# Attention over 32 graphs on one core: a schedule planned with other landings and durations, two plain projections and a fifth buffer

## The chip, the core and the metric

The kernel runs on one core of a Trainium2 chip. TensorE (PE) multiplies matrices into the eight PSUM banks, ScalarE (ACT) and VectorE (DVE) work on tiles in SBUF and read PSUM, GpSimd (POOL) and SyncE (SP) issue DMA transfers. Each engine runs its own queue of instructions strictly in order. The metric is the device time of one execution in microseconds, the median over several; lower is better.

## The reference

There are 32 graphs of 512 nodes with 512 features, each with an adjacency matrix of integers. For each graph the kernel computes a layer norm over the features and a ReLU, then two graph attention layers, and adds the input as residual. Layer 1 has four heads of 256 features, joined, with a bias and an ELU; layer 2 has one head of 512.

```
h   = relu(layernorm(x))
xl  = h @ W                                  # split into heads
e   = leaky_relu(xl·a_src [source] + xl·a_dst [target], 0.2)
att = softmax over sources of (e where adj > 0 or on the diagonal, else -1e9)
out = att^T @ xl + b
x + layer2(elu(layer1(h)))
```

All data are float32.

## The kernel before

The matrices are cut into 128 rows. Per graph and layer there are two matrix stages: the *projection* (`project1`: 512 x 512 by 512 x 1024; `project2`: 512 x 1024 by 1024 x 512, each with extra columns that give the attention scores) and the *gather* (attention weights times projected features).

**Block products.** Most of these products use a scheme with seven products of half-sized blocks instead of eight (`sevens`, L734, and `gather1`, L921). It needs sums of blocks ahead of the matmuls: `sums` (L693) makes four on DVE from the left operand (`ht` in layer 1, `h1` in layer 2), three of which lie in `hs`; `sums_of_weights` (L346) makes four of the weights, once, in slots 3 to 6 of `w1_sb` and `w2_sb`. One of them overwrites the weight block in slot 6. The results are put together after the matmuls: `minus` (L721) copies the first product of a block out of PSUM on ACT and subtracts the others on DVE. The first graph's `project1_first` (L797) and the first graphs' gathers (`gather1_plain`, L853) are plain: eight block products, that is a sum over all of the inner dimension in one PSUM bank, then one copy. With 258 columns a plain layer-1 projection is 64 matmuls where the other has 56; layer 2 has the same numbers at 257 columns.

**Softmax.** `Soft.columns` (L577) takes the score columns, spreads one of them over all partitions by two small DMAs through DRAM (`spread`: `das<-as`, `as<-das`). `Soft.first` (L596) makes, for four row tiles, a leaky ReLU on ACT, a masked minimum on DVE, an exponential with its sum on ACT; the logarithm of the sums goes through DRAM in the same way (`drr<-rr`, `rr<-drr`). `Soft.second` (L640) makes the weights `p` on DVE, adds the mask (by an accumulating DMA from POOL's queue, `p<-dm`, or by a DVE add for the first graph's first three heads and the last graph) and takes the exponential on ACT. The masks `m` are one tile; `masks` (L441) makes the next graph's after the last reader, and transposes them by DMA.

**Other steps.** `norm_turn` (L490) applies the norm on ACT and turns the tile: an ACT copy into an `adj` buffer, a DMA transpose, an ACT copy into `ht`. `elu` (L841) uses one tile of the buffers `xrs` (four of them, L297) for an exponential and a ReLU on ACT, then one DVE instruction writes `h1`. `residual` (L1012) loads x into `xrs` tiles and adds the bias b2 by an accumulating DMA; for graph 30, whose tiles lie elsewhere, by a DVE add with the copy of b2 in `b2_sb` (L287, L405). `gather2` (L1055) adds its products onto those tiles and writes them out.

**Order.** Nothing is issued as it is written. Every step is a job of class `Program` (L45) with an engine, a planned cost, what it reads and writes, and for a DMA its size. `order` (L169) plans with these costs: PE's jobs keep the order in which they are written; all other engines' jobs are ranked by how late they may run, found by planning backwards and forwards twelve times, and the plan with the earliest end is issued. A DMA of a size is planned to land after

```
landed = max(landed, t + jobs[j][1] + self.DMA_LEAD) + jobs[j][4] / self.DMA_RATE
r = landed + self.DMA_TAIL
```

with `DMA_LEAD, DMA_TAIL, DMA_RATE = 1.2, 1.0, 280e3` (L53; us, us, bytes per us). The planned order is fixed in the program; on the chip each engine waits at the head of its queue for what it needs.

The opening, in the order in which PE's jobs are written: `project1_first` for graph 0 (L1129), `project1` for graph 1 (L1146), the four heads of graph 0's gather (L1149), `project2` for graph 0 (L1163). The loop from L1169 then runs, per turn i, gather 1 of graph i+1 in two halves, `project1` of graph i+2 and gather 2 of graph i around it, and `project2` of graph i+1.

Of the kernel before, what the change touches and what calls it, by code (L numbers as in the profile page):

```python
# [10 lines left out]
F32 = mybir.dt.float32  # L11
# [8 lines left out]
P = 128  # L20
# [24 lines left out]
class Program:  # L45
# [6 lines left out]
    CROSS, SAME = 0.15, 0.1  # L52
    DMA_LEAD, DMA_TAIL, DMA_RATE = 1.2, 1.0, 280e3  # L53

# [155 lines left out]
def tile_gat(  # L210
# [75 lines left out]
    b1_sb = sbuf.tile([P, 2, FT], F32, name="b1_sb")  # L286
    b2_sb = sbuf.tile([P, DO], F32, name="b2_sb")  # L287
    part = sbuf.tile([P, 2, FT, 2], F32, name="part")
# [7 lines left out]
    adjs = slots("adj", 2, [P, N], I32)  # L296
    xrs = slots("xr", 4, [P, N])  # L297
    ls = slots("l", 3, [P, N])
# [95 lines left out]
    def weights2():  # L394

        for (r, c), ix in AT.items():
            dma(
                512e3, [("ht", 0, 0)], [("w2", ix)], w2_sb[:, ix, :, 1 - c : W2H - c],
                w2[r * HF // 2 : (r + 1) * HF // 2, c * DO // 2 : (c + 1) * DO // 2].rearrange(
                    "(k p) f -> p k f", p=P  # L400
                ),
            )
        dma(4e3, (), ["b1"], b1_sb[:, 0], b1.rearrange("(c p) -> p c", p=P))
        dve(TINY, ["b1"], ["b1"], nc.vector.tensor_scalar_mul, b1_sb[:, 1], b1_sb[:, 0], -1.0)
        dma(256e3, (), ["b2"], b2_sb, rows_of(b2, P))  # L405
        for a, v in enumerate((as2, ad2)):
            lk, bc = ls.take()
            dma(256e3, (), [lk], bc, rows_of(v[0], P))
            for (r, c), ix in AT.items():
                for k in range(KH):  # L410
                    jk, junk = xrs.take()
                    dve(
                        0.4, [lk, ("w2", ix)], [("part", a, r, c, k), jk],
                        nc.vector.scalar_tensor_tensor,
                        junk[:, : DO // 2], w2_sb[:, ix, k, 1 - c : W2H - c], 1.0,
                        bc[:, c * DO // 2 : (c + 1) * DO // 2], op0=OP.mult, op1=OP.mult,
                        accum_out=part[:, a, r * KH + k, c : c + 1],
                    )
                    xrs.give(jk)
            ls.give(lk)  # L420
        for a in range(2):
            for r in range(2):
                g = part[:, a, r * KH : (r + 1) * KH, :]
                col = slice(0, 1) if a == 0 else slice(W2H - 1, W2H)
                dve(
                    TINY, [("part", a, r, c, k) for c in range(2) for k in range(KH)],
                    [("w2s", AT[r, a])], nc.vector.tensor_add,
                    w2_sb[:, AT[r, a], :, col], g[:, :, 0:1], g[:, :, 1:2],
                )
# [60 lines left out]
    def norm_turn(b, t):  # L490
# [3 lines left out]
        act(  # L494
            0.62, [xk, sk + (t,)], [xk], hn, hn, AF.Relu,
            bias=st[:, t, S : S + 1], scale=st[:, t, S + A : S + A + 1],
# [13 lines left out]
        else:  # L510
# [3 lines left out]
            act(  # L514
                1.14, [xk], [ak], words.rearrange("p (h f) -> p h f", h=2),
                hn.bitcast(U16).rearrange("p (f h) -> p h f", h=2), AF.Copy,
# [9 lines left out]
            act(  # L526
                1.14, [xk], [("ht", t, 0), ("ht", t, 1)],
                ht[:, :, t * P : (t + 1) * P].bitcast(U16).rearrange("p k (n h) -> p h k n", h=2),
# [205 lines left out]
    def sevens(left, right, rkeys, put, kh, units, width, order):  # L734
# [3 lines left out]
        for u, n in order:  # L738
            m = units[u][0]
            acc, first = {1: "a", 2: "g", 5: "b", 6: "a", 7: "a", 3: "b", 4: "a"}[n], n in (1, 2, 5)  # L740
            if first:
# [4 lines left out]
            pe(  # L746
                akeys + rkeys(n), [bk], kh * width / 597,
                [
# [48 lines left out]
    def project1_first(zt):  # L797

        for j in range(H // 2):
            zk, z = zt[j]  # L800
            for t in range(NT):
                for c in range(2):
# [5 lines left out]
                           for q in (("w1", AT[r, c], k), ("w1s", AT[r, c], k, j))],  # L808
                        [bk], KT * 0.435,
                        [  # L810
# [9 lines left out]
                    banks.give(bk)  # L820
                yield

    def project1(b, left):
# [97 lines left out]
    def gather1(soft, j):  # L921
# [4 lines left out]
        for i, n in PAIR:  # L926
# [5 lines left out]
            if first:  # L932
# [4 lines left out]
            pe(  # L937
                akeys + wkeys, [bk], KQ * M / 597,
                [
# [37 lines left out]
    def project2(b, left):  # L977
# [18 lines left out]
        )  # L996

    def scores_2(b):
        def cols(z, i, zk):
# [12 lines left out]
    def residual(b, places=(xrs,) * NT):  # L1012

        XR[b] = []
        for d in range(NT):
# [6 lines left out]
            dma(256e3, (), halves, xr, x[b, d * P : (d + 1) * P, :])  # L1022
            if places[0] is xrs:
                accumulate(256e3, [xk], halves, xr, rows_of(b2, P))
            else:
                dve(0.59, [xk, "b2"], halves, nc.vector.tensor_add, xr, xr, b2_sb)
            XR[b].append((places[d], xk, xr))
# [74 lines left out]
    def run(products):  # L1102
        for _ in products:
            pass
# [7 lines left out]
    S1, S2 = {}, {}  # L1112
    PLAIN = 1
    HT_KEYS = [("ht", t, c) for t in range(NT) for c in range(2)]
# [13 lines left out]
    for t in range(NT):  # L1128
        norm_turn(1, t)  # L1129
    sums_of_weights(w1_sb, w1_keys, 1.2)  # L1130
    left1 = sums(ht_blocks(), KQ, 0.59)
    s = S1[0] = Soft(0, 1, lambda z, i, zk: [zk + (0, c, t) for c in range(2) for t in range(NT)])
# [9 lines left out]
    masks(1)  # L1142
    run(project1(1, left1))
    weights2()
# [15 lines left out]
    s.first(3)  # L1160
    sums_of_weights(w2_sb, lambda ix: [("w2", ix), ("w2s", ix)], 1.15)
    left2 = sums(h1_blocks(), KH, 1.15)
    run(project2(0, left2))  # L1163
    for t in range(NT):
# [98 lines left out]
```

## Time and profile before

| | us |
|---|---|
| median of 4 runs | 2869.75 (2866.93 to 2876.84) |
| the profiled execution | 2868.61 |
| its span | 2866.6 |
| TensorE busy | 2774.9 (97%) |
| VectorE busy | 2585.0 (90%) |
| ScalarE busy | 2305.6 (80%) |
| GpSimd busy | 417.7 (15%) |
| mean granted TensorE clock | 0.993 |

The profile shows one execution. "Busy" of TensorE includes matmuls that run at a lower granted clock. "Idle before" a group is the time in which its engine did nothing, and the releaser is what ended that time; names such as `mm<-w_sb,hs` read output from inputs, with buffer numbers left out (`mm` is a PSUM bank). All steps recorded by one helper carry one line: L316 is ACT, L319 DVE, L322 SP's DMAs, L327 POOL's accumulating DMAs, L333 the matmuls. A 128x512 tile of float32 is 256 KB.

### The profile page before, as it was taken

Reading aid. Unit: us, or ns where it says so; the run is one execution under the profiler, and the core shown is the slowest. Engines: PE = TensorE matmul, PEld = TensorE weight load, DVE = VectorE, ACT = ScalarE, POOL = GpSimd, SP = SyncE. Lnnn points to the kernel's source line nnn. Section 1 sums busy time; section 2 is a strip of 40 time slices with the busy share of each in tenths; the row PEclk is TensorE's granted clock in tenths of the full one; section 3 lists DMA queues with packets and bytes.
Section 4 is the critical chain, followed back from the end, with each engine's and each line's share of the span. In section 5 each row is a group of like instructions: output and inputs, shape, how many; then the busy total and the mean of one; then the engine's idle time right before and its main releaser. Section 6 shows DMA issues by size and latency. Waiting matters only on the chain. (4 is left out here: it accounts for less than half of the span.)

```text
span 2866.6 us, 41534 instructions
## 1 busy us (share of the span) xinstructions
PE 2774.9 (97%) x12456; PEld 2362.5 (82%) x12456; DVE 2585.0 (90%) x6567; ACT 2305.6 (80%) x4861; POOL 417.7 (15%) x466
## 2 busy tenths in 40 slices
PE   7999999999999999999999999999999999999997
PEld 6668888888888888888888878888888888888875
DVE  7979998989989989999989989999998999999995
ACT  6878797888878788887888778888888788888872
POOL 0011111111111111111111111111111111111100
PEclk9999999999999999999999999999999999999999
DMA  6577787687776777877787867778767788787724
GB/s 204 151 170 186 184 202 188 181 192 196 180 201 177 181 196 195 203 190 183 187 184 185 208 164 188 195 186 208 188 176 192 180 202 197 188 199 186 188 66 130
DMA packets 389455, 527.23 MB, mean 184 GB/s; under 512 B 227184, under 2 KB 231280, under 8 KB 389232
## 3 DMA queue, kind: packets, MB, share of 16 engines
q1 hardware_dynamic: 327600, 332.68, 41.6%
q0 software_dynamic: 61632, 191.92, 30.9%
q8 instruction: 99, 1.62, 0.2%
q14 instruction: 124, 1.02, 0.1%
HBM read 344.72 MB, written 50.79 MB: 138 GB/s over the span
## 5 line engine op out<-in xcount | busy, mean ns | idle before, releaser
L333 PE MATMUL mm<-w_sb,hs 128*128 128x257 f32 (+1 forms) x3024 | 694.1, 383 | 23.6 <-ACT xl L316 14.8
L333 PEld LDWEIGHTS mm<-w_sb,hs 128*128 128x128 f32 x3024 | 572.8, 191 | 119.8 <-ACT xl L316 26.9
L327 POOL DMA_DIRECT2D p<-dm x304 | 268.1, 883 | 2046.2 <-DVE p L319 1030.4
L316 ACT ACTIVATE l<-as,z 128x512 f32<-128x512 f32 x640 | 441.8, 723 | 111.4 <-DMA as<-das 103.5
L316 ACT ACTIVATE p<-p,z 128x512 f32<-128x512 f32 x640 | 432.7, 722 | 112.1 <-DMA p<-dm 78.5
L316 ACT ACTIVATE l<-l,low 128x512 f32<-128x512 f32 x640 | 459.4, 723 | 72.3 <-DVE low L319 70.4
L319 DVE SCALAR_TENSOR_TENSOR p<-rr,z 128x512 f32<-128x512 f32 x640 | 457.6, 744 | 45.3 <-DMA rr<-drr 45.0
L333 PE MATMUL mm<-p,xl 128*128 128x256 f32 (+1 forms) x2016 | 488.5, 390 | 7.3 <-ACT p L316 5.9
L333 PE MATMUL mm<-w_sb,ht 128*128 128x258 f32 x2112 | 481.5, 382 | 4.1 <-ACT xl L316 3.1
L333 PE MATMUL mm<-w_sb,h 128*128 128x257 f32 x2056 | 470.0, 380 | 6.3 <-DVE h L319 4.3
L319 DVE CUSTOM_DVE_ANT_1 l<-l,mt 128x512 f32<-128x512 f32 x640 | 426.8, 682 | 42.8 <-ACT l L316 40.6
L333 PEld LDWEIGHTS mm<-w_sb,ht 128*128 128x128 f32 x2112 | 400.4, 190 | 66.1 <-ACT xl L316 6.1
L333 PEld LDWEIGHTS mm<-p,xl 128*128 128x128 f32 x2016 | 381.7, 190 | 83.9 <-issue 19.1
L333 PEld LDWEIGHTS mm<-w_sb,h 128*128 128x128 f32 x2056 | 389.9, 190 | 65.7 <-DVE h L319 5.3
L316 ACT ACTIVATE xl<-mm 128x258 f32<-128x258 f32 (+2 forms) x752 | 282.1, 384 | 54.3 <-PE mm L333 52.2
L319 DVE TENSOR_TENSOR xl<-xl,mm 128x258 f32<-128x258 f32 x558 | 224.1, 417 | 34.6 <-PE mm L333 25.6
L316 ACT ACTIVATE h<-mm 128x256 f32<-128x256 f32 x480 | 175.1, 379 | 76.5 <-PE mm L333 75.9
L316 ACT ACTIVATE xr<-h,b_sb 128x512 f32<-128x512 f32 x240 | 171.5, 723 | 80.9 <-DVE h L319 80.5
L333 PE MATMUL mm<-t,hs 128*128 128x256 f32 x960 | 217.7, 379 | 0.9 <-DVE hs L319 0.7
L333 PEld LDWEIGHTS mm<-t,hs 128*128 128x128 f32 x960 | 182.1, 190 | 26.7 <-DVE hs L319 1.1
L319 DVE TENSOR_TENSOR xr<-mm,xr 128x256 f32<-128x256 f32 (+1 forms) x424 | 170.6, 416 | 32.2 <-PE mm L333 19.3
L319 DVE SCALAR_TENSOR_TENSOR h<-h,b_sb,xr 128x512 f32<-128x512 f32 x240 | 175.7, 744 | 19.8 <-ACT xr L316 19.0
(105 smaller groups left out, 3427.3 us busy)
## 6 DMA issues: line engine op xcount, KB each, us to landing
p<-dm POOLq DMA_DIRECT2D x304, 512.0 KB, 5.1
rr<-drr SPq DMA_DIRECT2D x160, 512.0 KB
x<-in_x_dram SPq DMA_DIRECT2D x129, 256.0 KB
adj<-in_adj_dram SPq DMA_DIRECT2D x128, 256.0 KB
as<-das SPq DMA_DIRECT2D x64, 512.0 KB
xr<-in_x_dram SPq DMA_DIRECT2D x124, 256.0 KB
xr<-in_L_gnn_b_dram POOLq DMA_DIRECT2D x124, 256.0 KB, 6.0
out_dram<-xr SPq DMA_DIRECT2D x124, 256.0 KB
```

Of the source, the lines that this page charges most:

```text
L316: prog.add("ACT", cost, reads, writes, lambda: nc.scalar.activation(*a, **k))
L319: prog.add("DVE", cost, reads, writes, lambda: f(*a, **k))
L327: lambda: nc.gpsimd.dma_start(to, at, accum_op=OP.add), 1.4 * size,
L333: f(*a, **k)
```

## The change

- `DMA_TAIL` is 1.3 instead of 1.0, and the planned costs of three ACT steps and of the matmuls are other numbers.
- Graph 1's layer-1 projection and graph 0's layer-2 projection are plain: `project1_plain` and `project2_plain`. The block sums of `ht` and `h1` for these two go; the sums of the weights are written after them.
- `b2_sb` is gone, with its load; `residual` adds b2 by an accumulating DMA for every graph. `xrs` has five tiles instead of four.

```diff
-    DMA_LEAD, DMA_TAIL, DMA_RATE = 1.2, 1.0, 280e3
+    DMA_LEAD, DMA_TAIL, DMA_RATE = 1.2, 1.3, 280e3
...
-    b2_sb = sbuf.tile([P, DO], F32, name="b2_sb")
...
-    xrs = slots("xr", 4, [P, N])
+    xrs = slots("xr", 5, [P, N])
...
-        dma(256e3, (), ["b2"], b2_sb, rows_of(b2, P))
...
-            0.62, [xk, sk + (t,)], [xk], hn, hn, AF.Relu,
+            0.71, [xk, sk + (t,)], [xk], hn, hn, AF.Relu,
...
-                1.14, [xk], [ak], words.rearrange("p (h f) -> p h f", h=2),
+                0.96, [xk], [ak], words.rearrange("p (h f) -> p h f", h=2),
...
-                1.14, [xk], [("ht", t, 0), ("ht", t, 1)],
+                1.21, [xk], [("ht", t, 0), ("ht", t, 1)],
...
-                akeys + rkeys(n), [bk], kh * width / 597,
+                akeys + rkeys(n), [bk], kh * width / 593,
...
-                        [bk], KT * 0.435,
+                        [bk], KT * 0.437,
...
+    def project1_plain():
+
+        for j in range(H // 2):
+            for c in range(2):
+                h = 2 * j + c
+                for t in range(NT):
+                    bk, bt = banks.take()
+                    pe(
+                        [("ht", t, 0), ("ht", t, 1)]
+                        + [q for r in range(2) for k in range(KQ)
+                           for q in (("w1", AT[r, c], k), ("w1s", AT[r, c], k, j))],
+                        [bk], KT * 0.437,
+                        [
+                            (mm, (bt[:, :W], ht[:, k, t * P : (t + 1) * P],
+                                  w1_sb[:, AT[k // KQ, c], k % KQ, j, :]),
+                             dict(start=(k == 0), stop=(k == KT - 1)))
+                            for k in range(KT)
+                        ],
+                    )
+                    act(
+                        COPY, [bk], [("xl", t, h, i) for i in range(FPH)], xl[:, t, h, :], bt[:, :W],
+                        AF.Copy, scale=-1.0,
+                    )
+                    banks.give(bk)
...
-                akeys + wkeys, [bk], KQ * M / 597,
+                akeys + wkeys, [bk], KQ * M / 593,
...
+    def project2_plain():
+
+        for t in range(NT):
+            for c in range(2):
+                bk, bt = banks.take()
+                for k in range(FT):
+                    ix = AT[k // KH, c]
+                    pe(
+                        [("h1", k, t // 2), ("w2", ix), ("w2s", ix)], [bk], 0.437,
+                        [(mm, (bt[:, :W2H], h1[:, k, t * P : (t + 1) * P], w2_sb[:, ix, k % KH, :]),
+                          dict(start=(k == 0), stop=(k == FT - 1)))],
+                    )
+                act(
+                    COPY, [bk], [("xl2", t, c)], xl2[:, t, c * W2H : (c + 1) * W2H], bt[:, :W2H],
+                    AF.Copy, scale=-1.0,
+                )
+                banks.give(bk)
...
-            if places[0] is xrs:
-                accumulate(256e3, [xk], halves, xr, rows_of(b2, P))
-            else:
-                dve(0.59, [xk, "b2"], halves, nc.vector.tensor_add, xr, xr, b2_sb)
+            accumulate(256e3, [xk], halves, xr, rows_of(b2, P))
...
-    PLAIN = 1
+    PLAIN, PLAIN_A, PLAIN_C = 1, True, True
...
-    sums_of_weights(w1_sb, w1_keys, 1.2)
-    left1 = sums(ht_blocks(), KQ, 0.59)
+    if not PLAIN_A:
+        sums_of_weights(w1_sb, w1_keys, 1.2)
+        left1 = sums(ht_blocks(), KQ, 0.59)
...
-    run(project1(1, left1))
+    if PLAIN_A:
+        project1_plain()
+    else:
+        run(project1(1, left1))
...
-    left2 = sums(h1_blocks(), KH, 1.15)
-    run(project2(0, left2))
+    w2_keys = lambda ix: [("w2", ix), ("w2s", ix)]
+    if PLAIN_C:
+        project2_plain()
+        sums_of_weights(w2_sb, w2_keys, 1.15)
+    else:
+        sums_of_weights(w2_sb, w2_keys, 1.15)
+        left2 = sums(h1_blocks(), KH, 1.15)
+        run(project2(0, left2))
+    if PLAIN_A:
+        sums_of_weights(w1_sb, w1_keys, 1.2)
```

More of the change, by code (lines that the diff above doesn't have):

```diff
@@ L1160, in tile_gat @@
     s.first(3)
-    sums_of_weights(w2_sb, lambda ix: [("w2", ix), ("w2s", ix)], 1.15)
-    left2 = sums(h1_blocks(), KH, 1.15)
-    run(project2(0, left2))
+    w2_keys = lambda ix: [("w2", ix), ("w2s", ix)]
[8 more added lines that the diff above has]
+        sums_of_weights(w1_sb, w1_keys, 1.2)
     for t in range(NT):
```

## The prediction

> **What bounds the kernel now.** I read the busy table first, then TensorE's waits, its timeline in the opening, the windows by stage, and last the waits on transfers.
>
> ```profile
> PE 2774.9 (97%) x12456; PEld 2362.5 (82%) x12456; DVE 2585.0 (90%) x6567; ACT 2305.6 (80%) x4861; POOL 417.7 (15%) x466
> ...
> 0.00:200.00 200.00, 171.85 (x629) 123.34 (x630) 152.71 (x470) 147.25 (x300) 18.12 (x25) 0.96 0.68 173
> 200.00:2740.00 2540.00, 2495.95 (x11387) 2155.73 (x11386) 2337.71 (x5889) 2102.05 (x4440) 390.87 (x431) 1.00 0.75 189
> 2740.00:2866.60 126.60, 107.14 (x444) 83.39 (x442) 94.53 (x210) 56.29 (x122) 8.71 (x10) 0.97 0.35 94
> ```
>
> TensorE is the bound with 91.7 us idle in the span: 28.15 in the first 200 us, 44.05 in the next 2540, 19.5 in the last 127. Faster work elsewhere pays only if it ends one of these waits.
>
> ```profile
> 51.10 3.81 PE L333 MATMUL mm<-w_sb,hs 128*128 128x258 f32 x8 [6.12 <-DVE hs L319]
> 70.99 2.88 PE L333 MATMUL mm<-w_sb,hs 128*128 128x258 f32 x12 [1.48 <-ACT xl L316]
> 78.93 7.03 PE L333 MATMUL mm<-p,w_sb 128*128 128x512 f32 x16
> 106.39 3.72 PE L333 MATMUL mm<-w_sb,h 128*128 128x257 f32 x16
> 114.37 3.79 PE L333 MATMUL mm<-w_sb,h 128*128 128x257 f32 x8 [4.26 <-DVE h L319]
> 124.16 1.90 PE L333 MATMUL mm<-w_sb,h 128*128 128x257 f32 x8
> 138.07 13.89 PE L333 MATMUL mm<-p,xl 128*128 128x512 f32 x32
> ```
>
> The columns are start, duration, group, and the idle time before it with its releaser. One matmul is two records here. The waits of 6.12 and 4.26 us are for block sums, and the eight records after each take 3.81 and 3.79 us where eight normally take 1.90: a long wait is paid again in clock.
>
> ```profile
> PE mm L333 <- DVE xr L319: 14.7, 20, 3.0
> PE mm L333 <- DVE hs L319: 13.3, 5, 3.5
> PE mm L333 <- ACT xl L316: 11.4, 17, 1.4
> ...
> ACT l L316 <- DMA as<-das: 103.5, 34, 6.1
> ACT p L316 <- DMA p<-dm: 78.5, 52, 6.8
> ...
> DVE p L319 <- DMA rr<-drr: 45.0, 43, 4.7
> ...
> p<-dm POOLq DMA_DIRECT2D x304, 512.0 KB, 5.1
> ```
>
> The first three are TensorE's waits between 200 and 2740 us, the next three the whole span's waits on transfers (total, times, longest). ACT and DVE run a fixed order, so a transfer that lands later than planned holds up what stands behind it, bank copies among them.
>
> **The change part by part.** The sum is against the profiled execution, 2866.6 us of span and 2868.6 us in all; that is 1.1 us under the median of 2869.75.
>
> *Graph 1's projection, plain.* 64 matmuls instead of 56: 8 at 0.44 us (128 records in 28.11 us) are +3.5. Gone: the wait of 6.12, its slow clock of 1.9, and the waits of 0.44, 0.58 and 1.48 behind it: -10.5. Also gone from DVE, fully busy from 60 to 109 us, are 4 block sums (0.60 each) and 12 subtractions (0.34): 6.5 us. Three of the four weight sums still stand early in DVE's order; the fourth (1.14 us) now stands among graph 0's last ELUs, and graph 2's projection, which reads it, began at 151.81: hidden. New: the 16 products fill the eight PSUM banks, and in ACT's new order 26 instructions stand between the first and the second bank copy: 13 leaky ReLUs at 0.61, 10 exponentials at 0.70, a layout copy at 1.22, two small ones, 16.3 us. TensorE ends graph 0's projection at about 43.2 (120 of the 128 records from 16.87), the first copy ends near 45.3, so the second ends near 62.0; TensorE wants that bank for its tenth group at 43.2 + 9 x 1.75 = 58.9. That is a wait of 3.1, and about 1 of clock (after the 3.00 us wait at 816 us four records took 1.96 us for 1.03). The first gather, at 78.93 before, can then start near 75.4. Its exponentials follow 45 ACT instructions in the new order, 24.8 us at the trace's rates from 45.3, so they are done near 74 to 75. I take **-3.4**; bounds -7.6 (no wait: 71.3) and +0.6 (twice the wait).
>
> *Graph 0's second projection, plain.* Before: 31.7 us (106.39 to 138.07) for 56 matmuls worth 24.4; the rest is the wait of 4.26 and 3.1 us of clock. After: 64 at 0.435 are 27.8, and no block sums of h1 stand before them (four of 1.14 us). The one weight sum that moves behind it is read by graph 1's second projection, which began at 207.62: hidden, as long as DVE gets to it within 70 us. The first group needs the last ELU at its eighth matmul, 3.0 us in. That ELU took 7.9 us in the old order (its exponential started at 110.33, the result at 113.57); in the new one its exponential has one leaky ReLU ahead of it, so 3 to 5 us. I take 1 us of wait, **-2.9**; bounds -3.9 (no wait) and +1.5 (the old wait and some clock).
>
> *What is late next.* TensorE would be at graph 1's gather 6.3 us earlier, at 131.8, where it had no wait but no slack either: the exponentials it needs began at 135.53 and 138.43. They follow a chain through DVE. I priced DVE's instructions from graph 0's first row of p to the spread for this head at the trace's rates: 53.0 us in the old order and 48.2 in the new. That row waits for a spread through DRAM (62.51 before) and starts no earlier, so the chain comes 4.8 us earlier: **+1.5** given back; bounds 0 and +6.3.
>
> *Landings and durations in the plan.* These reorder everything after 200 us; TensorE's own order there is unchanged. Every altered constant moves to the trace: ReLU 0.62 to 0.71 (trace 0.71 apart), layout copies 1.14 to 0.96 and to 1.21 (0.95 and 1.20 apart), a 256-wide matmul 0.429 to 0.432 (0.4325). The masks' transfer was planned as 1.2 + 700/280 + 1.0 = 4.7 us, now 5.0; the row says 5.1. The 44.05 us of middle waits and some 7 of clock are at stake. ACT's 98 waits on transfers average 2.0 us (with 12.6 for x<-adj), DVE's 43 on rr 1.05; 0.3 us is 15 and 29% of these. I take the lower share of 51: **-8**. It is the least certain term: below, half of it goes (-26); above, two new waits like that at 458.73 (3.48 us, then 6.65 for 16 records that take 3.62: 6.5 in all), +13. The fifth xr buffer, from the row of b2 copies, lies inside this term: it can only let a residual row's load start earlier, and the xr waits are 14.7 us in all. The load of that copy (256 KB, issued by SP at 13.4 us) goes too: at the 296 GB/s of the first 20 us it is 0.9 us that graph 1's x rows gain, but TensorE has graph 0's projection to do until 43.2; hidden, at most -0.9.
>
> Here the Trainium skill speaks against the change. "DMA: Bandwidth & Descriptors", section "Anatomy of one DMA", puts such a transfer at about 2.0 us and its bytes at 436 GB/s, some 3.2 us for 512 KB as an estimate. By that the old plan was already too late and this term would be nothing, making 2863 of the sum; the row's 5.1 us decides.
>
> *The end.* Graph 30's residual takes b2 by accumulating DMA: four DVE adds (0.68 each) go, four POOL issues (0.86) come. Two of the adds ran at 2715, one at 2807.1, and the chain that ended last runs through DVE from 2730 to 2779, so some of them lay before it. On POOL's queue the last of the new transfers stands ahead of the masks of graph 30's p. Its x row was issued by SP at 2804.24 and had landed by 2807.1, the masks' transfers began at 2814.33: 7 us of cover; without it DVE's sums of that p, at 2825.53, would slip, and 0.39 us later in its queue stands the last graph's path. I take **-1**; bounds -2.7 (all four on the path) and +1. The last gather still waits for the last graph's softmax (8.02 us before 2847.19).
>
> Sum: -3.4 - 2.9 + 1.5 - 8 - 1 = -13.8, hence 2854.8, **2855 us**.
>
> **The rivals.**
> *Given back (0.14).* The opening's 4.8 us do not last, as graph 1's heads come just in time, and the reorder is neutral: about -1 to -4, 2866. For it: at 164.6 ACT stood 6.81 us for a mask transfer with the DMA engines 98% busy, and TensorE 3.95 at 181; nothing cut removes that. Against: priced in the same way, DVE has 12 us less to do before graph 1's first p (87.3 for 99.5).
> *Middle waits halve (0.18).* -26 in place of -8, and 2837. For it: seven waits of over 1.5 us make 19 of the 44. Against: DVE stays 92% busy there, with little room.
> *Slower (0.22).* Work fed by transfers is now placed later in DVE's queue; where the transfer was on time, block sums come late instead. Each costs 6.5 us as at 458.73 and 1690.76. From three more on they outweigh the other terms by over 0.3% (+19.5 - 5.8 = +13.7), 2882; two make +7.2. For it: those two waits sit behind DVE at 92%. Against: landings in the trace exceed even the new plan's.
> *The forecast (0.46)*: 2846 to 2861.
>
> **How the numbers follow.** Measurement tells about 0.3%, 8.6 us, from no change. Faster: 0.18 and 0.42 of the forecast's 0.46, 0.60. Within: 0.14 and 0.04, 0.18. Slower: 0.22. The range runs from the halved waits, less some opening, to three new waits: 2834 to 2881.
>
> **What would show it.** No wait near 45 us, one of about 3 us near 59 on a bank copy, the first gather near 75.4, no wait of over 2 us at the second projection's start, graph 1's gather near 133. Between 200 and 2740, some 36 us of idle instead of 44, and ACT's waits on as and dm below 182. The last gather's wait near 8 us still. I am wrong if new waits of 3 us on block sums turn up in the middle, or if graph 1's gather still starts at 138.

## The result, and the profile after

The changed kernel takes 2876.66 us (median of 38 runs, 2864.74 to 2897.24) beside 2870.04 us for the kernel before (median of 59, 2854.68 to 2881.3). The ratio is 1.0035, 95% interval 1.0023 to 1.0046: slower by a third of a per cent, where 0.5% faster was forecast. The profiled execution took 2877.37 us, its span is 2875.5 us, and the mean granted clock 0.991.

The busy table of the changed kernel, TensorE's row, and then its windows by stage (columns as before: stretch, its length, busy time and records of PE, PEld, DVE, ACT and POOL, granted clock, DMA share, GB/s):

```profile
PE 2789.8 (97%) x12488; PEld 2372.7 (83%) x12488; DVE 2571.0 (89%) x6537; ACT 2305.9 (80%) x4861; POOL 426.2 (15%) x470
```

```profile
0.00:200.00 200.00, 182.10 (x698) 132.61 (x699) 146.96 (x456) 149.10 (x303) 19.07 (x26) 0.99 0.67 177
200.00:2740.00 2540.00, 2490.74 (x11341) 2149.82 (x11340) 2326.78 (x5864) 2097.44 (x4433) 395.82 (x431) 0.99 0.76 188
2740.00:2875.50 135.50, 116.91 (x453) 90.30 (x451) 97.27 (x219) 59.39 (x126) 11.36 (x13) 0.91 0.39 105
```

TensorE is idle for 17.9 us in the first 200 us (28.15 before), for 49.3 us in the middle (44.05 before, 36 forecast) and for 18.6 us at the end, where its granted clock is 0.91 instead of 0.97. DVE is less busy than before, by 14 us, and it did not help. Over the whole span TensorE idles 85.7 us, 6.0 less than before (91.7), but it is busy for 14.9 us more. The 16 more matmuls of the plain products are about 7 us of that (32 records at 0.22); the other 8 are matmuls that took longer, in line with the mean granted clock, 0.991 for 0.993.

The opening, TensorE's timeline of the changed kernel:

```profile
53.75 24.57 PE L332 MATMUL mm<-w_sb,ht 128*128 128x258 f32 x104 [4.10 <-ACT low L315]
78.16 7.03 PE L332 MATMUL mm<-p,w_sb 128*128 128x512 f32 x16
...
105.63 28.25 PE L332 MATMUL mm<-w_sb,h 128*128 128x257 f32 x128
134.60 14.21 PE L332 MATMUL mm<-p,xl 128*128 128x512 f32 x32 [0.72 <-ACT p L315]
...
199.78 5.38 PE L332 MATMUL mm<-w_sb,h 128*128 128x257 f32 x24
```

and ACT's, between the first two bank copies of graph 1's projection:

```profile
46.20 0.39 ACT L315 ACTIVATE xl<-mm 128x258 f32<-128x258 f32 x1 [1.36 <-PE mm L332]
...
52.37 1.33 ACT L315 ACTIVATE ht<-x 128x1024 uint16<-128x1024 uint16 x1
...
62.87 0.37 ACT L315 ACTIVATE xl<-mm 128x258 f32<-128x258 f32 x1
```

Both plain products do what they should. The waits of 6.12 and 4.26 us on block sums are gone, graph 1's gather starts at 134.60 (138.07 before) and its second projection at 199.78 (207.62 before). At this point the changed kernel is 7.8 us ahead.

The lead does not last. The table takes the start of a graph's second projection as a milestone, in us from the span's start:

| second projection of | before | after | after is ahead by |
|---|---|---|---|
| graph 1 | 207.6 | 199.8 | 7.8 |
| graph 2 | 292.6 | 292.2 | 0.4 |
| graph 18 | 1704.3 | 1686.3 | 18.0 |
| graph 30 | 2731.9 | 2733.9 | -2.0 |
| graph 31 | 2790.8 | 2799.9 | -9.1 |
| end of the span | 2866.6 | 2875.5 | -8.9 |

One undisturbed turn takes 85.0 us (207.6 to 292.6 before). The lead comes and goes by whole waits: two kernels whose matmuls past the opening are the same are 18.0 us apart one way at graph 18 and 9.1 us the other way at graph 31. What takes it away, in the changed kernel's waits (total, times, longest): first those of TensorE from 200 to 2740 us, then the waits of ACT and DVE on transfers over the whole span.

```profile
PE mm L332 <- DVE hs L318: 24.2, 15, 5.5
PE mm L332 <- DVE xr L318: 8.0, 15, 2.5
PE mm L332 <- ACT xl L315: 5.6, 6, 1.9
PE mm L332 <- ACT h L315: 5.3, 10, 1.6
PE mm L332 <- ACT p L315: 4.9, 5, 2.4
...
ACT l L315 <- DMA as<-das: 115.1, 40, 5.2
ACT p L315 <- DMA p<-dm: 73.8, 43, 5.8
DVE p L318 <- DMA rr<-drr: 29.7, 27, 3.4
```

Waits on block sums (`hs`) went from 13.3 us in 5 waits to 24.2 in 15; those on `xr` and `xl` fell by 12.5 us together. The waits on `as` and `dm` together are 188.9 us (182.0 before, and forecast to fall). Three of the waits on block sums are over 3 us, at 632.71 (4.07), 858.11 (3.30) and 1730.84 (5.47); the two of that size before (3.48 at 458.73 and 3.44 at 1690.76) are gone. How they come about, in the changed kernel's timeline before 858.11, TensorE first, then DVE, ACT, POOL's issues and SP's, and last SP's wait for a transfer between 848 and 857 us:

```profile
858.11 4.24 PE L332 MATMUL mm<-w_sb,hs 128*128 128x258 f32 x12 [3.30 <-DVE hs L318]
...
857.36 0.69 DVE L318 TENSOR_TENSOR hs<-ht 128x512 f32<-128x512 f32 x1 [2.30 <-ACT ht L315]
...
852.34 1.33 ACT L315 ACTIVATE p<-p,z 128x512 f32<-128x512 f32 x2 [2.79 <-DMA p<-dm]
...
855.99 1.33 ACT L315 ACTIVATE ht<-x 128x1024 uint16<-128x1024 uint16 x1
...
843.58 0.86 POOL L326 DMA_DIRECT2D p<-dm  x1 [0.96 <-PE mm L332]
...
844.58 4.00 SPq L519 DMA_TRANSPOSE x<-adj  x1
...
854.84 0.81 SPq L321 DMA_DIRECT2D adj<-in_adj_dram  x2
...
SPq L321 <- DMA x<-adj: 5.1, 1, 5.1
```

POOL issued the masks' transfer of a head at 843.58, and SP the DMA transpose of a tile of a later graph at 844.58. ACT stood 2.79 us for the masks, to 852.34, and then worked without a gap through bank copies, ReLUs and exponentials to the layout copy into `ht` at 855.99. DVE stood 2.30 us for that copy, and TensorE 3.30 us for the block sum of it. The copy and the sum belong to the later graph and need neither the masks nor that head: they stand behind them in ACT's order. But the masks are the smaller part. The copy reads the transposed tile, and SP's queue tells when that had landed: SP held its next load of the `adj` buffer back 5.1 us for the transpose, to 854.84. Without the masks ACT would have come to the copy at 853.2 and stood there until about 854.8. So about 1.2 of the 3.30 us belong to the masks, the rest to the transpose.

At 1730.84 the masks cost nothing in the end:

```profile
1723.79 1.33 ACT L315 ACTIVATE p<-p,z 128x512 f32<-128x512 f32 x2 [3.66 <-DMA p<-dm]
...
1728.72 1.34 ACT L315 ACTIVATE ht<-x 128x1024 uint16<-128x1024 uint16 x1 [1.04 <-DMA x<-adj]
```

ACT stood 3.66 us for masks, but then 1.04 more at the layout copy for the DMA transpose of that very tile. At 632.71 the block sum is one of `p`, whose exponential had waited for its own masks. So in all three a transfer that the sum itself needs was late. The plan has a transpose land 4.5 us after its issue at the earliest (1.3 of cost, 1.2, 200/280 and 1.3); these two took 10.2 us (from 844.58) and 11.5 (from 1717.20).

The slow records after each wait make it dearer. The 24 records from 1730.84 took 8.36 us where 24 such take 5.38, and the three waits cost 8.5, 6.6 and 4.8 us with this (surplus of 3.0, 2.5 and 1.5 us).

The granted clock from 1730.8 to 1740 is 0.68. The Trainium skill ("TensorE: Matmul & The Clock Gate", section "Part 1: The HAM clock gate (the 'warmup' mystery)") has the array at half clock after an idle window of about 3.4 us until it has been busy for about as long; worked out from that, a long wait would cost an estimated 1.7 us more. The slow records behind the three waits here cost 1.5 to 3.0. And shorter waits do it too, as TensorE's timeline near the end of the changed kernel shows, where four such records take 1.13 us behind a wait of 0.48 and 2.08 behind one of 1.85:

```profile
2778.23 1.13 PE L332 MATMUL mm<-p,xl 128*128 128x256 f32 x4 [0.48 <-ACT p L315]
2781.21 2.08 PE L332 MATMUL mm<-p,xl 128*128 128x256 f32 x4 [1.85 <-ACT p L315]
```

### The profile page after: what moved, and what is told of

Same layout as the page of the kernel before. It is cut to its first block, busy times and chain, and to the rows that moved or that the text cites. A ratio compares the mean times of both kernels' runs of the same rounds, so it can differ in the third digit from the quotient of the medians.

```text
span 2875.5 us, 41541 instructions
## 1 busy us (share of the span) xinstructions
PE 2789.8 (97%) x12488; PEld 2372.7 (83%) x12488; DVE 2571.0 (89%) x6537; ACT 2305.9 (80%) x4861; POOL 426.2 (15%) x470
## 5 line engine op out<-in xcount | busy, mean ns | idle before, releaser
L332 PE MATMUL mm<-w_sb,hs 128*128 128x258 f32 (+1 forms) x2928 | 671.2, 383 | 17.8 <-DVE hs L318 13.5
L332 PEld LDWEIGHTS mm<-w_sb,hs 128*128 128x128 f32 x2928 | 557.0, 191 | 108.1 <-DVE hs L318 15.9
L332 PE MATMUL mm<-w_sb,ht 128*128 128x258 f32 x2176 | 496.8, 383 | 8.4 <-ACT low L315 4.1
L332 PE MATMUL mm<-w_sb,h 128*128 128x257 f32 x2120 | 481.5, 379 | 0.0
L332 PEld LDWEIGHTS mm<-w_sb,ht 128*128 128x128 f32 x2176 | 413.2, 190 | 72.8 <-ACT xl L315 4.5
L332 PEld LDWEIGHTS mm<-w_sb,h 128*128 128x128 f32 x2120 | 401.1, 189 | 60.3 <-DVE h L318 0.6
L315 ACT ACTIVATE xl<-mm 128x258 f32<-128x258 f32 (+2 forms) x752 | 281.0, 382 | 58.9 <-PE mm L332 57.2
L318 DVE TENSOR_TENSOR xl<-xl,mm 128x258 f32<-128x258 f32 x540 | 216.3, 417 | 35.4 <-PE mm L332 31.3
L315 ACT ACTIVATE xr<-h,b_sb 128x512 f32<-128x512 f32 x240 | 170.4, 721 | 92.3 <-DVE h L318 91.7
L326 POOL DMA_DIRECT2D xr<-in_L_gnn_b_dram x124 | 114.0, 960 | 513.5 <-DMA xr<-in_x_dram 492.7
```

What stands on the lines that cost most here:

```text
L315: prog.add("ACT", cost, reads, writes, lambda: nc.scalar.activation(*a, **k))
L318: prog.add("DVE", cost, reads, writes, lambda: f(*a, **k))
L326: lambda: nc.gpsimd.dma_start(to, at, accum_op=OP.add), 1.4 * size,
L332: f(*a, **k)
```

## The experiments

Three theories went into the first runs. A: the opening's lead is real and lasts, and the later landing loses more than that. B: every altered constant draws a fresh order of ACT, DVE and the DMA queues, and the waits of the middle are drawn anew with it, whatever the part is meant to do. C: the opening's lead is given back.

All ratios are to the kernel before, run on the same chip beside them. The table is a summary of what follows. "Planned end" is what the kernel's own planner (`order`) works out for the plan that it issues; it is no measurement. "hs" is the total of TensorE's waits on block sums between 200 and 2740 us, in the profiled execution.

| kernel | ratio (95%) | planned end, us | hs, us |
|---|---|---|---|
| before | 1 | 2787.4 | 13.3 |
| before, landing 1.001 | 1.0026 (1.0011 to 1.0041) | 2802.4 | 18.6 |
| before, landing 0.999 | 1.0067 (1.0051 to 1.0082) | 2798.0 | 13.9 |
| before, landing 1.3 | 0.9905 (0.9878 to 0.9932) | 2794.2 | 8.3 |
| before, landing 1.299 | 0.9999 (0.9983 to 1.0016) | 2805.6 | 19.3 |
| before, landing 1.301 | 1.0015 (0.9998 to 1.0032) | 2808.4 | 13.1 |
| before, opening plain | 0.9962 (0.9942 to 0.9983) | 2794.6 | 11.1 |
| before, new durations | 0.9946 (0.9927 to 0.9965) | 2786.5 | 6.5 |
| before, b2 by DMA and fifth tile | 0.9976 (0.9952 to 1.0001) | 2781.3 | 5.6 |
| after | 1.0035 (1.0023 to 1.0046) | 2799.0 | 24.2 |
| after, landing 1.301 | 1.0039 (1.0021 to 1.0058) | 2802.0 | 22.8 |
| after, landing 1.299 | 0.9955 (0.9938 to 0.9972) | 2795.7 | 12.7 |
| after, landing 1.0 | 0.9985 (0.9966 to 1.0004) | 2780.3 | 8.9 |
| after, old durations | 0.9903 (0.9880 to 0.9925) | 2774.0 | 3.5 |
| after, opening in sevens | 0.9948 (0.9930 to 0.9967) | 2797.6 | 18.1 |
| after, b2 by DVE and four tiles | 0.9910 (0.9885 to 0.9934) | 2797.2 | 7.4 |
| before, 60 rounds | 0.9871 (0.9846 to 0.9896) | 2766.5 | no such wait |
| before, 60 rounds, landing 1.001 | 0.9869 (0.9846 to 0.9892) | 2765.7 | 0.7 |
| after, 60 rounds | 0.9848 (0.9821 to 0.9875) | 2783.1 | 5.4 |
| after, 60 rounds, landing 1.301 | 0.9907 (0.9885 to 0.9930) | 2782.7 | 7.2 |

### Each part alone

The opening (and nothing else of the change) on the kernel before:

```diff
-    PLAIN = 1
+    PLAIN, PLAIN_A, PLAIN_C = 1, True, True
...
-    run(project1(1, left1))
+    if PLAIN_A:
+        project1_plain()
...
-    run(project2(0, left2))
+    if PLAIN_C:
+        project2_plain()
...
```

> Only the two plain products are taken over; the old landings, durations and buffers stay (b2 stays a DVE add). Theory A (the opening's lead is real and lasts, the planner's new constants lost the time): graph 1's second projection starts near 200 us instead of 207.6 and the whole is 5 to 8 us faster than before, ratio 0.997 to 0.998. Theory B (every new plan is a fresh order whose middle waits are drawn anew, several us either way): the second projection near 200, but the total anywhere from 0.997 to 1.004, with waits of TensorE at other places than before. Theory C (the lead is given back because ACT and DVE set the pace after 200 us): the third projection, at 292.6 before, starts within 2 us of that, and the ratio is 0.999 to 1.001.

The landing:

```diff
-    DMA_LEAD, DMA_TAIL, DMA_RATE = 1.2, 1.0, 280e3
+    DMA_LEAD, DMA_TAIL, DMA_RATE = 1.2, 1.3, 280e3
```

> Only the planned tail of a landing goes from 1.0 to 1.3 us. Theory A (later landings put work that waits for transfers later, and block sums come late): slower by 5 to 12 us, ratio 1.002 to 1.004, with more and longer waits of TensorE on hs, ACT's waits on as and p transfers shorter. My forecast's own step: faster by about 5 us, ratio 0.998. Theory B (fresh draw): 0.997 to 1.004, and the waits' places bear no relation to transfers.

The durations:

```diff
-            0.62, [xk, sk + (t,)], [xk], hn, hn, AF.Relu,
+            0.71, [xk, sk + (t,)], [xk], hn, hn, AF.Relu,
...
-                akeys + rkeys(n), [bk], kh * width / 597,
+                akeys + rkeys(n), [bk], kh * width / 593,
```

and the other four of the change in the same way.

> Only the planned durations of the ReLU, the two layout copies and the matmuls are changed to the measured ones. Theory A (it is the landings that lose): same or faster, ratio 0.998 to 1.000. Theory B (fresh draw): 0.997 to 1.004. If the durations are the part that loses, 1.002 or more here and not in the landings alone.

b2 and the fifth tile:

```diff
-    b2_sb = sbuf.tile([P, DO], F32, name="b2_sb")
...
-    xrs = slots("xr", 4, [P, N])
+    xrs = slots("xr", 5, [P, N])
...
-            if places[0] is xrs:
-                accumulate(256e3, [xk], halves, xr, rows_of(b2, P))
-            else:
-                dve(0.59, [xk, "b2"], halves, nc.vector.tensor_add, xr, xr, b2_sb)
+            accumulate(256e3, [xk], halves, xr, rows_of(b2, P))
```

> Only b2_sb goes and xr has five tiles, b2 being added by accumulating DMA for graph 30 too. My forecast's step: -1 us at the end, waits on xr (14.7 us between 200 and 2740 before) 8 to 12 us, ratio 0.998 to 1.000. Theory B (fresh draw): 0.997 to 1.004.

Measured, with 2868.78 us for the kernel before: the opening 2856.50, the landing 2843.92, the durations 2852.76, b2 and the fifth tile 2861.70 us. By the medians each is faster, by 12, 25, 16 and 7 us: 60 us together, where the whole change is 7 us slower. The last is not clear of no change (its interval reaches 1.0001), and its waits on `xr` fell to 9.2 us, as expected. A falls, since the landing alone is the fastest of the four, and so does C for the opening alone: it was 13.1 us ahead at graph 1's second projection and still 17.2 at graph 30's. Its timeline on TensorE is close to the good end of what was forecast for graph 1's projection, a wait of 0.37 us and the first gather at 72.53:

```profile
49.80 22.89 PE L333 MATMUL mm<-w_sb,ht 128*128 128x258 f32 x104 [0.37 <-ACT ht L316]
72.53 7.03 PE L333 MATMUL mm<-p,w_sb 128*128 128x512 f32 x16
...
105.70 25.05 PE L333 MATMUL mm<-w_sb,h 128*128 128x257 f32 x114 [1.78 <-DVE h L319]
```

### Each part left out

If the parts were terms of a sum, leaving one out of the changed kernel would cost its gain. There was a rival for the end as well: from the start of graph 30's second projection to that of graph 31 the kernel before took 58.9 us, the changed one 66.0 and b2 with the fifth tile alone 66.3, so these might cost 5 to 7 us there.

The edits are those above, taken back one at a time:

```diff
-    DMA_LEAD, DMA_TAIL, DMA_RATE = 1.2, 1.3, 280e3
+    DMA_LEAD, DMA_TAIL, DMA_RATE = 1.2, 1.0, 280e3
```

> The changed kernel with the old 1.0 us landing back in the planner's constants. If the parts were terms of a sum, taking the landing out would lose its 25 us and give about 2902 us (2877 + 25). Fresh plans (each altered constant gives a new order of ACT, DVE and the DMA queues, whose waits in the middle stand in no relation to the ones before): anywhere from 2844 to 2880, and it is as likely to end below the changed kernel as above. The tail theory (the b2 transfers and the fifth xr tile cost 5 to 7 us in the last two stages): the stretch from the start of graph 30's second projection to the start of the last graph's stays near 66 us, where the kernel before had 58.9.

```diff
-            0.71, [xk, sk + (t,)], [xk], hn, hn, AF.Relu,
+            0.62, [xk, sk + (t,)], [xk], hn, hn, AF.Relu,
```

> The changed kernel with the old durations (0.62, 1.14, 1.14, 597, 0.435) in the plan. Terms of a sum: 2877 + 16 = about 2893 us. Fresh plans: 2844 to 2880. The tail theory: still near 66 us from graph 30's second projection to the last graph's, since the b2 transfers and the fifth tile are in.

```diff
-    PLAIN, PLAIN_A, PLAIN_C = 1, True, True
+    PLAIN, PLAIN_A, PLAIN_C = 1, False, False
```

> The changed kernel with graph 0's and graph 1's products in the seven-product form of before. Terms of a sum: 2877 + 12 = about 2889 us. Fresh plans: 2844 to 2880, with the second projection of graph 0 starting near 109 us and the lead of the opening gone, whatever the total. The tail theory: still near 66 us in the last stage but one.

```diff
-    xrs = slots("xr", 5, [P, N])
+    xrs = slots("xr", 4, [P, N])
...
-            accumulate(256e3, [xk], halves, xr, rows_of(b2, P))
+            if places[0] is xrs:
+                accumulate(256e3, [xk], halves, xr, rows_of(b2, P))
+            else:
+                dve(0.59, [xk, "b2"], halves, nc.vector.tensor_add, xr, xr, b2_sb)
```

> The changed kernel with four xr tiles and b2 added by DVE for graph 30, as before. Terms of a sum: 2877 + 7 = about 2884 us. The tail theory: the stretch from graph 30's second projection to the last graph's goes back from 66 to about 60 us, and the total to about 2865 to 2871 if the middle stays as it is. Fresh plans: the tail says nothing of the total, 2844 to 2880.

Measured, with 2868.44 for the kernel before: 2865.68 without the landing, 2844.53 without the durations, 2853.03 without the plain opening, 2841.18 without b2 by DMA and the fifth tile. By the ratios each is faster than the changed kernel, by 0.5 to 1.3%, whichever part is missing. The sum of terms expected 2884 to 2902 us and falls in all four. The rival for the end does not show in these runs: with b2 on DVE and four tiles that stretch took 65.2 us, and without the landing, but with five tiles, 60.5. It is not settled either. Over all twenty kernels the stretch is 64.5 us on average with five tiles (60.3 to 66.7) and 61.2 with four (58.9 to 65.2): the two overlap, but the means are 3.2 us apart, three times the uncertainty of that difference. A planned landing near 1.3 goes with five tiles in most of the kernels and parts them as well (64.2 us in eleven, 60.8 in nine). Which of the two lengthens the end, and by how much, these runs do not tell.

### A thousandth of a microsecond

B says that any change of a constant does as much as any other. The planned landing was moved by 0.001 us in both kernels, which no engine can feel:

```diff
-    DMA_LEAD, DMA_TAIL, DMA_RATE = 1.2, 1.0, 280e3
+    DMA_LEAD, DMA_TAIL, DMA_RATE = 1.2, 1.001, 280e3
```

> The kernel before with the planned landing of a transfer at 1.001 us in place of 1.0. Nothing that the chip can feel is changed but the order: by the theory that the parts have worths of their own (terms of a sum), one thousandth of a microsecond is worth nothing, and the time is 2868 to 2870 us, as before, within 4. By the theory that every change of a planner's constant draws a fresh order whose waits are drawn anew: anywhere between 2840 and 2880, the spread of the eight partial kernels and the two given ones (2841 to 2877, mean 2856); being far above that mean, the kernel before has 2 chances in 3 to get faster by more than 4 us.

With 0.999 in its place:

> The kernel before with the planned landing at 0.999 us. Terms of a sum: 2868 to 2870 us within 4, and the same as the kernel with 1.001. Fresh order: anywhere between 2840 and 2880, and no nearer to the kernel with 1.001 than to any other.

```diff
-    DMA_LEAD, DMA_TAIL, DMA_RATE = 1.2, 1.3, 280e3
+    DMA_LEAD, DMA_TAIL, DMA_RATE = 1.2, 1.301, 280e3
```

> The changed kernel with the planned landing at 1.301 us in place of 1.3. Terms of a sum (including any clash between the parts that is a property of what the change does): 2877 us within 4, slower than the kernel before. Fresh order: anywhere between 2840 and 2880, mean 2856, so most likely faster than the kernel before by 10 us or so; then the changed kernel's +7 us belongs to the one order that its constants drew and not to its parts.

With 1.299 in its place:

> The changed kernel with the planned landing at 1.299 us. Terms of a sum: 2877 us within 4. Fresh order: anywhere between 2840 and 2880. In both dithers of the changed kernel the opening is held to start its second projections of graph 0 and graph 1 about as early as in the changed kernel (100 to 106 and 194 to 200 us), since that lead comes from the products and not from the order; if it is gone, the opening too is a matter of the order.

Measured, with 2863.27 for the kernel before beside them: 2869.87 (1.001), 2880.53 (0.999), 2871.51 (1.301) and 2848.56 us (1.299). TensorE's order is the same in each pair, and the others' orders are not. The kernel before moves by 0.67% on a thousandth of a microsecond, the changed one by 0.84% between 1.299 and 1.301. The forecast that the kernel before would get faster, being above the mean of the others, missed: both its neighbours are slower.

The same row of TensorE's waits, 200 to 2740 us, in the changed kernel with 1.301 and then with 1.299:

```profile
PE mm L332 <- DVE hs L318: 22.8, 16, 4.3
```

```profile
PE mm L332 <- DVE hs L318: 12.7, 11, 2.1
```

Ten microseconds less of waiting for block sums go with 23 us less of time. The two profiled executions have spans of 2872.5 and 2842.9 us; their busy rows:

```profile
PE 2782.7 (97%) x12488; PEld 2371.5 (83%) x12488; DVE 2574.7 (90%) x6537; ACT 2302.8 (80%) x4861; POOL 424.8 (15%) x470
```

```profile
PE 2772.1 (98%) x12488; PEld 2369.4 (83%) x12488; DVE 2571.3 (90%) x6537; ACT 2303.3 (81%) x4861; POOL 423.7 (15%) x470
```

Of the 29.6 us between them TensorE idled 19.0, and for the other 10.6 the same 12488 records took longer. Over the twenty kernels of the table the row on block sums correlates with the ratio at 0.79, and all of TensorE's idle time between 200 and 2740 us at 0.86, so block sums are one kind of wait among several: with the opening in sevens they were waited for 18.1 us, and the ratio is 0.9948. That is what the traces show; no run changed one wait alone.

The opening's lead does not hold in every order either. In these two orders of the changed kernel graph 1's second projection starts at 205.37 (1.301) and 203.16 us (1.299), where 194 to 200 was expected.

The mean of the three orders of the kernel before is 1.0031, that of the changed kernel's three is 1.0010. Sixteen orders that were planned with twelve rounds have a standard deviation of 0.0050 (14 us), so a mean of three is known to about 0.003 (0.0050 over the root of 3). The scatter is not that of the parts: the three groups of three in the table that differ by a thousandth alone have 0.0048 between them. The parts of the change have no worth that can be told from nothing here, and the +0.35% is one order's.

### The landing again

The landing alone had the largest gain, 25 us. Is that its own or its order's?

```diff
-    DMA_LEAD, DMA_TAIL, DMA_RATE = 1.2, 1.0, 280e3
+    DMA_LEAD, DMA_TAIL, DMA_RATE = 1.2, 1.299, 280e3
```

> The kernel before with only the planned landing changed, to 1.299 us. With 1.3 it took 0.9905 of the kernel before. If the later landing has a worth of its own (fewer waits on transfers: 165 us with 1.3 for 227), this gives 0.986 to 0.996 too, 2825 to 2855 us. If the 25 us were only the luck of that one order: anywhere from 2840 to 2880, mean 2856 (0.9955), as likely above as below.

With 1.301:

> The same with 1.301 us. A worth of its own: 2825 to 2855 us, ACT's and DVE's waits on as, dm and rr together below 190 us. Luck of the order: 2840 to 2880, those waits anywhere from 160 to 258 us, and the time following them.

Measured, with 2868.93 before: 2869.09 and 2873.04 us. So nearly all of the 25 us belonged to that one order. The mean of the three is 0.9973, beside 1.0031 for the three with a landing near 1.0; the difference of 0.0058 is 1.4 times its uncertainty (0.0050 x the root of 2/3), which is not enough to call it shown. The waits on `as`, `dm` and `rr` did fall, to 184.8 and 180.0 us (227.0 before, 165.4 with 1.3), as a truer landing should make them (though the kernel before with 1.001 has 187.7), but that did not carry over to the time: the first of the two waits 19.3 us for block sums, the second 13.1, and the lucky one 8.3. Over all sixteen orders with twelve rounds, the nine with a landing near 1.3 have a mean of 0.9968 and the seven near 1.0 one of 0.9995: 8 us apart, with an uncertainty of 7.

### More rounds

The planner stops after twelve rounds and issues the plan with the earliest end. For the kernel before the best plan was the twelfth, and the ends were still falling (2807.6, 2796.9, 2794.5, 2787.4 us in the last four). So its order is a point on a noisy path and not the end of it. The constants as they are, with more rounds:

```diff
-    ROUNDS = 12
+    ROUNDS = 60
```

> The kernel before with the planner's rounds raised from 12 to 60: the same constants, jobs and products, and the best of 60 orders instead of 12. The end that the planner itself gives falls from 2787 to 2766 us. If an order's own planned end decides: 21 us less, about 2845 us. If the order is drawn blind: 2840 to 2880.

> The changed kernel with 60 rounds: its own planned end falls from 2799 to 2783 us. If the planned end decides: 16 us less, about 2861 us, and slower than the kernel before with 60 rounds (planned 2766). If later landings make the plan come truer, as the orders so far hint (planned with 1.3 us they took on average 60 us more than planned, with 1.0 us 75): 2783 + 60 = 2843, level with 2766 + 75 = 2841. If the order is drawn blind: 2840 to 2880.

Measured: 2832.01 us for the kernel before with 60 rounds and 2825.06 for the changed one, 37 and 44 us less than the 2868.93 of the kernel before, and less than every number expected. And with the same thousandth of a microsecond on top (`DMA_TAIL` 1.001 and 1.301):

> The kernel before with 60 rounds of the planner and the planned landing at 1.001 us: its planned end is 2765.7 us (2802.4 with 12 rounds). If 60 rounds make the plan better, and not one lucky order: again 0.980 to 0.992 of the kernel before, where the same constant with 12 rounds gave 1.0026. If the two results with 60 rounds were luck: 2840 to 2880 us (0.990 to 1.004).

> The changed kernel with 60 rounds and 1.301 us: planned end 2782.7 us (2802.0 with 12 rounds, measured 1.0039). If 60 rounds make the plan better: 0.980 to 0.992. If the changed parts are worth something once the plan is settled, this is below the kernel before with 60 rounds and 1.001 us by about 7 us, as 2825 stands to 2832; if not, the two orders of each kernel overlap.

Measured, with 2867.40 before: 2830.04 and 2838.95 us. So it is not the luck of two orders. The four have a mean of 0.9874, sixteen orders with twelve rounds 0.9979; three of the four lie below all sixteen, the fourth among their best. In the middle (200 to 2740 us) the waits of TensorE are now, first in the kernel before with 60 rounds and then in the changed kernel with 60 rounds:

```profile
PE mm L333 <- ACT h L316: 12.6, 14, 3.2
PE mm L333 <- DVE xr L319: 6.5, 12, 1.6
PE mm L333 <- ACT xl L316: 4.7, 10, 1.4
PE mm L333 <- ACT p L316: 0.6, 1, 0.6
```

```profile
PE mm L332 <- ACT h L315: 9.2, 11, 2.8
PE mm L332 <- ACT p L315: 8.1, 7, 2.8
PE mm L332 <- DVE hs L318: 5.4, 5, 3.1
PE mm L332 <- DVE xr L318: 3.8, 6, 1.4
PE mm L332 <- ACT xl L315: 2.7, 5, 1.1
```

The row on block sums is gone from the one and down to 5.4 us in the other. The windows of the changed kernel with 60 rounds show 29.2 us of idle TensorE in the middle:

```profile
200.00:2740.00 2540.00, 2510.80 (x11488) 2178.16 (x11486) 2360.58 (x5952) 2123.16 (x4496) 393.86 (x433) 1.00 0.76 190
```

With 60 rounds the two orders of the kernel before stand at 0.9871 and 0.9869, those of the changed kernel at 0.9848 and 0.9907, around them on both sides: here, too, the change's parts have no worth that can be told. The planner's own end put the changed kernel 17 us behind (2783 against 2766), and that is not what was measured.

## Why the prediction was wrong

The step that failed is the term "Landings and durations in the plan", -8, with the sentence "Every altered constant moves to the trace" as its reason. It took truer constants for a gain, and left out that any altered constant draws a new order of ACT, DVE and the DMA queues. By the milestones this stretch, from graph 1's second projection to graph 30's, took 9.8 us more than before (from 7.8 ahead to 2.0 behind) in place of 8 less. A new order alone does as much: a thousandth of a microsecond in one constant moved the changed kernel by 23 us. Beside a draw with a standard deviation of 14 us, 8 us can't be read from one order. Whether truer constants gain anything on average is not shown: over the sixteen orders the later landing stands 8 us lower, with an uncertainty of 7, and the new durations 3 us. The bounds of -26 to +13 for this term, 39 us or 2.8 standard deviations, were about as wide as such a draw. The next term failed as well, *The end*: 6.9 us more (from 2.0 behind to 8.9) in place of 1 less.

Point by point:

- *Graph 1's projection*, -3.4 expected: the wait of 6.12 us went, but the forecast wait on a bank copy did not come. ACT ran the second copy at 62.87, to 63.24 (62.0 forecast), and TensorE did not stand for it. It stood earlier, 4.10 us from 49.65 to 53.75, when it had three groups of graph 1 behind it: the fourth needs the last tile of `ht`, and ACT's layout copy of that tile ran from 52.37 to 53.70. (The timeline names `low`, a small ACT instruction that ended at the same time; in the two orders below it names `ht`.) The prediction had this copy in its list of 26 instructions, as one that delays the bank copy, and left out that TensorE needs it. Its own numbers give the wait: nine instructions ahead of the copy are 5.9 us, so it ends at 45.3 + 5.9 + 1.2 = 52.4, and the fourth group was due at 43.2 + 3 x 1.75 = 48.5, 3.9 us earlier. That the forecast wait was of about this size is luck. The first gather began at 78.16, 0.8 us earlier than before instead of 3.5. In the orders with a wait of 0.37 or 0.60 us there (the opening alone, and the change without b2 by DMA and the fifth tile) it began at 72.53 and 72.75. All three lie inside the bounds.
- *Graph 0's second projection*, -2.9 expected: it took 28.25 us against 31.68 before, -3.4; the 1 us of wait that was put in for the last ELU did not come.
- *Given back*, +1.5 expected: 0.72 us of waiting at graph 1's gather in this order. The three terms make -4.8; they were -0.8, -3.4 and +0.7, and the gather came 3.5 us earlier. Over all kernels graph 1's second projection starts at 199.6 us on average with the plain products (nine orders, 193.4 to 209.4) and at 204.5 without (eleven, 201.4 to 211.1): -4.8 us. On average the size was right, with an uncertainty of 2.0 us; in a single order it is buried, and the wait inside it was another.
- *The middle*: 36 us of idle forecast, 49.3 measured. The rival "Slower" named the kind of wait that came: block sums late, 6.5 us each. Three new ones over 3 us cost 8.5, 6.6 and 4.8 us, 6.6 on average, and the condition under which the prediction called itself wrong ("new waits of 3 us on block sums turn up in the middle") is met. But two as large went, so it is one more and not three, and the rest of the growth is in short ones. And the reason was another: the transfers that these sums need were late themselves, which the rival had excluded ("where the transfer was on time"); work placed ahead of a sum cost 1.2 us at one of the three. The change does not bring these waits by itself either, since with 1.299 us none is over 2.1 us and the ratio is 0.9955.
- *The end*, -1 expected: the stretch from graph 30's second projection to graph 31's took 7.1 us longer. b2 by DMA with the fifth tile is not shown to be the cause (65.2 us without it in one order, 60.5 with it in another), and not cleared: on average over the twenty kernels five tiles go with 3.2 us more here, a landing near 1.3 with 3.4.
- *The range and the chances*: 2834 to 2881 held the time. Of the other fifteen orders with twelve rounds seven are faster than the kernel before by over 0.3%, five within, and three slower: 0.47, 0.33 and 0.20, which is what a fresh draw would have been worth here, in place of 0.60, 0.18 and 0.22.

What stays open, beside the end: why a plan after 60 rounds has fewer late block sums. Its planned end is 16 to 37 us earlier with the same constants, but across the sixteen twelve-round orders the planned end goes with the ratio at 0.47 only, and the changed kernel's plans, 17 us later than those of the kernel before, are as fast. An order with one such sum moved by hand was not tried.

## What to carry to other kernels

When a planner writes a fixed order, every edit of a cost, a buffer or a job draws a new order; before a part is credited with a gain or a loss, move a constant by a thousandth and see how far the time goes by itself. Here that was 0.5% (one standard deviation), as much as the four parts seemed to gain alone (0.2 to 1.0%), and each of them seemed to lose in company. See first whether the planner has settled: 60 rounds instead of 12 were worth 1.0%, more than truer landings and durations showed.

## What the runs showed of the hardware

The masks' transfers take longer from issue to landing with five `xr` tiles and b2 by DMA. The rows of transfers in the changed kernel and in the same kernel without that part (the last column is the median in us):

```profile
p<-dm POOLq DMA_DIRECT2D x304, 512.0 KB, 5.6
```

```profile
p<-dm POOLq DMA_DIRECT2D x304, 512.0 KB, 5.2
```

In the nine kernels with the part it is 5.3 to 5.7 us, mean 5.5; in the eleven without it 5.0 to 5.4, mean 5.2. POOL's queue, from which the masks are issued too, also stands longer for the x rows of the residual: 423 to 554 us in all with the part, 221 to 329 without. The prediction had said that the buffer "can only let a residual row's load start earlier", and had put no cost on it. What the 0.3 us cost was not measured apart; the ratios do not show it.
